# First graph layer: the score row taken by a block transpose on VectorE and a trip through DRAM instead of transposes on TensorE

## The chip, the cores and the metric

The kernel runs on one core of a Trainium2 chip. The metric is the time of one execution on the device, in microseconds (us). The kernel before takes 2509.26 us, the median of three runs (2508.89 to 2510.26 us).

## The reference

`x` is 64 graphs of 256 nodes with 512 features, all float32; `adj` is one 256 x 256 adjacency matrix for all graphs. Two layers follow each other, each with a residual:

```python
h = relu(layernorm(x)); x = x + layer0(h, adj)     # graph attention, 1 head
h = relu(layernorm(x)); x = x + layer1(h, adj)     # multi-head attention, 8 heads of 64

# layer0, per graph (W: 512 x 256, a: 2 x 256)
h  = X @ W
e  = (h @ a[0]) + (h @ a[1]).T         # a column plus a row: 256 x 256 scores
e  = leaky_relu(e, 0.2); masked softmax over neighbours -> alpha
out = concat([alpha @ h, h])
```

The change concerns `e` of the first layer: the sum of a column (a number per node, on the partitions) and a row (the same number of the other nodes, along the free dimension and equal on all partitions).

## The kernel before, in words

**Work units.** Two graphs make a group `g`; there are 32 groups (`NG`). A group has four tiles of 128 nodes (`GT = 4`), two per graph. The kernel is a software pipeline written out by hand: while the attention of group `g` runs (two halves, `b = 0` and `b = 1`, one per graph), the projections q, k, v of group `g+1` and the first layer of group `g+2` are fed into TensorE between its pieces. Each of these is a Python generator; one call of `next` emits one piece. The strings in `steps` say in which order the pieces are emitted: `S` scores of the second layer, `m` a mask of two heads, `u` one projection product (eight TensorE instructions of 256 columns pairwise, a piece of `project`), `o` an output product (`py`, a piece of `outputs`), `s` a piece of `first_layer`, `n` a piece of `first_norm` (the layernorm and transpose of a later group). TensorE follows this order exactly. For the other engines `not_sooner` ties an instruction to the one before it on its engine; where it is not used, a scheduler may place the instruction sooner or later.

**The first layer.** `first_layer(g)` has 14 pieces. Four pieces compute the head product `ph` of a tile: `h` with two more columns for the two scores; ScalarE copies it to `H` (`scalar.copy(H[:, r, : F1 + 2], ph)`), GpSimd adds it to the residual. The fifth piece makes the scores: four TensorE transposes into a PSUM tile `pn`, each of one column of `H` broadcast to 128 columns, which gives the row on all partitions; then four ScalarE instructions that add the column to it (`e<-pn,H`, 128 x 256), one leaky ReLU per graph on VectorE (`SCALAR_TENSOR_TENSOR e<-e`) and one exponential per graph on ScalarE (`ACTIVATE e<-e`). The sixth piece masks `e` on VectorE, the next four are the products `po`, and the last four normalise for the second layer.

**The order of one group's first half.** With `b = 0` the string is `Smmnuuuumonmuouuossnunosunosnouso`. Its last three pieces are a projection product `u`, the score piece `s` (`pn` and `e`), and an output product `o`. Then `weigh` of the half follows: eight products `total` (softmax sums), two VectorE reciprocals `r<-total`, two blocks `pr` of sixteen products, the products `oT` of `pr` and `r` on VectorE; and then the scores `sc` of the next half, eight banks of two products each, written in pairs and read by eight ScalarE exponentials `p<-sc`.

**PSUM.** Eight banks: three are held by name (`held_bank`), and five form the pool `turn` from which `mm` takes a bank for every other product. A product that takes a bank must wait until the bank's last reader is done. `ph`, `pn`, `total`, `pr`, `sc`, `po` and the second banks of the projections and outputs all come from these five. Which of the five a product gets is fixed when the program is built.

**Queues.** All loads and stores are issued by SyncE, one queue, in program order: an issue that waits holds the later ones. The first layer's norm already sends its tiles through DRAM (`passed`, `moved`). `r`, the tile of the reciprocals, has one buffer (`bufs=1`).

```python
for quad in range(NQ):
    not_sooner(vector, "reciprocal", r[:, quad, :], total[:, quad, :])
```

Of the kernel before, what the change touches and what calls it, by code (L numbers as in the profile page):

```python
# [8 lines left out]
F32 = mybir.dt.float32  # L9
I32 = mybir.dt.int32  # L10
AF = mybir.ActivationFunctionType
# [3 lines left out]
P = 128  # L15
# [26 lines left out]
def two_gnn_layers(tc, *args):  # L42

    nc = tc.nc
    with tc.tile_pool(name="verdict", bufs=1) as pool:
        wrong = pool.tile([1, 1], I32, name="wrong")
        bounded(tc, *args, wrong)  # L50
        again = nc.values_load(wrong[0:1, 0:1], min_val=0, max_val=1)
        with tc.If(again > 0):
            tc.strict_bb_all_engine_barrier()
            any_inputs(tc, *args)
# [3 lines left out]
def bounded(  # L58
# [23 lines left out]
    nc = tc.nc  # L82
    vector, scalar, gpsimd, sync = (
        Remembers(e) for e in (nc.vector, nc.scalar, nc.gpsimd, nc.sync)
    )
    B, N, D = x.shape
# [3 lines left out]
    NT = N // P  # L90
    GB = 2
    GT = GB * NT
    TOK = GB * N
# [3 lines left out]
    S = 32  # L97
# [4 lines left out]
    att = ctx.enter_context(tc.tile_pool(name="att", bufs=2))  # L102
    small = ctx.enter_context(tc.tile_pool(name="small", bufs=6))
    psum = ctx.enter_context(tc.tile_pool(name="psum", bufs=1, space=bass.MemoryType.PSUM))
    dram = ctx.enter_context(tc.tile_pool(name="dram", bufs=4, space=bass.MemoryType.DRAM))
# [3 lines left out]
    def mm(name):  # L109
        return psum.tile([P, 512], F32, tag="turn", name=name, bufs=5)  # L110
# [4 lines left out]
    def after(instruction, name):  # L115

        tc.add_manual_dep(
            instruction.ins, name,
            mybir.DependencyInfo(mybir.DependencyClass.NoSync, mybir.DependencyReason.DATA),
            reason="the engine's order",  # L120
        )

    def not_sooner(engine, operation, *args, **kwargs):

        last = engine.last
        after(getattr(engine, operation)(*args, **kwargs), last)
# [4 lines left out]
    def in_order(instruction):  # L131
        if before:
            after(instruction, before.pop())
        before.append(instruction.ins.name)

    def matmul(*args, **kwargs):
        in_order(nc.tensor.matmul(*args, **kwargs))  # L137

    def transpose(*args):
        in_order(nc.tensor.transpose(*args))  # L140
# [17 lines left out]
    ident = const.tile([P, P], F32, name="ident")  # L158
# [238 lines left out]
    def stats(mv, src, t, name):  # L397
        st = small.tile([P, 6], F32, tag="st", name=f"st{name}_{t}", bufs=4)
        if vector.last:
            not_sooner(vector, "bn_stats", st, src[t])  # L400
        else:
            vector.bn_stats(st, src[t])
        vector.bn_aggr(mv[:, t, :], st)
# [69 lines left out]
    def operand_sums(engine, quads, sums):  # L473
        a11, a12, a21, a22 = quads
        not_sooner(engine, "tensor_add", sums[:, 0], a21, a22)
        engine.tensor_sub(sums[:, 1], sums[:, 0], a11)

        not_sooner(engine, "tensor_sub", a21, a11, a21)
        engine.tensor_sub(sums[:, 2], a12, sums[:, 1])

    def seven(quads, sums):

        a11, a12, s3, a22 = quads
        s1, s2, s4 = (sums[:, i] for i in range(3))
        return {
            1: (a11, W11), 2: (a12, W21), 3: (s4, W22), 4: (a22, T4),
            5: (s1, T1), 6: (s2, T2), 7: (s3, T3),  # L490
        }
# [41 lines left out]
    H = const.tile([P, GT, F1 + 3], F32, name="H")  # L533
    gpsimd.memset(H[:, :, F1 + 2 :], 1.0)

    def first_layer(g):

        xt = [xs[g, b][:, t, :] for b in range(GB) for t in range(NT)]
        for r in range(GT):
            b, t = divmod(r, NT)  # L540
            ph = mm(f"ph_{g}_{r}")[:, : F1 + 2]
            for c in range(HP):
                matmul(
                    ph, hT0[g, b][:, c, t * P : (t + 1) * P], w0_sb[:, c, :],
                    start=(c == 0), stop=(c == HP - 1),
                )
            scalar.copy(H[:, r, : F1 + 2], ph)
            gpsimd.tensor_add(xt[r][:, F1:], H[:, r, 2 : F1 + 2], xt[r][:, F1:])
            yield

        pn = mm(f"pn_{g}")
        for t in range(GT):
            transpose(pn[:, t * P : (t + 1) * P], H[:, t, 0:1].to_broadcast([P, P]), ident)
        pT = {}
        for b in range(GB):
            e = att.tile([P, NT, N], F32, tag="e", name=f"e_{g}_{b}")
            for kb in range(NT):
                scalar.activation(
                    e[:, kb, :], pn[:, b * N : (b + 1) * N], AF.Identity,
                    bias=H[:, b * NT + kb, 1:2], scale=1.0,  # L560
                )
            vector.scalar_tensor_tensor(e, e, ALPHA, e, op0=ALU.mult, op1=ALU.max)
            scalar.activation(e, e, AF.Exp)
            pT[b] = e
        if g:
            yield
        for b in range(GB):
            not_sooner(vector, "tensor_mul", pT[b], pT[b], maskT)
        yield
        if g == 0:  # L570
            yield
        mv = small.tile([P, GT, 2], F32, tag="mv", name=f"mv1_{g}", bufs=4)
        factors, norm, turn, fetch, put = norm_T(xt, mv, f"1_{g}", g == 0)
        row_factors = small.tile([P, GT], F32, tag="ri", name=f"ri_{g}", bufs=2)
        for r in range(GT):
            b, t = divmod(r, NT)
            po = mm(f"po_{g}_{r}")[:, : F1 + 1]
            for kb in range(NT):
                matmul(
                    po, pT[b][:, kb, t * P : (t + 1) * P], H[:, b * NT + kb, 2:],  # L580
                    start=(kb == 0), stop=(kb == NT - 1),
                )
            ri = row_factors[:, r : r + 1]
            not_sooner(vector, "reciprocal", ri, po[:, F1:])
            vector.scalar_tensor_tensor(
                xt[r][:, :F1], po[:, :F1], ri, xt[r][:, :F1], op0=ALU.mult, op1=ALU.add
            )
            stats(mv, xt, r, f"1_{g}")
            if r == 1:
                factors(0)  # L590
            elif r == 2:
                norm(0)
            elif r == 3:
                factors(1)
                if g:
                    turn(0)
                    fetch(0)
            yield
        hT = big.tile([P, HP, TOK], F32, tag="hT1", name=f"hT1_{g}")
        sums = big.tile([P, 3, 2, N], F32, tag="sums", name=f"sums_{g}", bufs=1)  # L600
        quads = [
            hT[:, 2 * c : 2 * c + 2, r * N : (r + 1) * N] for r in range(2) for c in range(2)
        ]
        operands[g] = seven(quads, sums)
        if g == 0:
            turn(0)
            put(0, hT[:, :, :N])
            yield
        norm(1)
        yield  # L610
        turn(1)
        fetch(1)
        yield
        if g:
            put(0, hT[:, :, :N])
            yield
        put(1, hT[:, :, N:])
        operand_sums(gpsimd, quads, sums)
        yield
# [218 lines left out]
    for piece in range(5):  # L838
        next(norms)
        if piece == 3:  # L840
            score_columns()
            next(edges)
    products, pieces = project(0), first_layer(1) if NG > 1 else iter(())
    for piece, _ in enumerate(first_layer(0)):
        if piece == 1:
            next(norms)
            next(norms)
            next(edges)
        elif piece == 2:
            next(norms)  # L850
        elif piece == 3:
            next(norms)
            late_loads()
        elif piece == 4 or piece == 9:
            next(verdict)
        elif piece == 10:
            next(verdict)
            next(verdict)
            next(norms)
            next(norms)  # L860
            weight_sums("q")
        elif piece == 11:
            next(products)
            next(products)
# [18 lines left out]
    run(verdict)  # L883


    steps = ("Smmnuuuumonmuouuossnunosunosnouso", "Ssmmususuososmuomssusuonusonuouunous")
    waiting, late = None, iter(())
    for g in range(NG):
        products = project(g + 1) if g + 1 < NG else iter(())
        pieces = first_layer(g + 2) if g + 2 < NG else iter(())  # L890
        for b, parts in enumerate(steps):
            if g == b == 0:
# [401 lines left out]
```

## Time and profile before

| | |
|---|---|
| median of three runs | 2509.26 us |
| the profiled execution: time, and span in the trace | 2508.17 us, 2506.5 us |
| TensorE busy | 2473.7 us (99%) |
| VectorE, ScalarE, GpSimd busy | 1684.0, 1009.8, 1018.9 us |
| DMA, mean share of its engines, by tenths | 2 to 3 tenths in most slices |
| length of one group in the middle of the run | 76.4 us |

Busy time counts an engine's instructions; a wait shows in the profile as idle time before an instruction, with the engine that ended it. The chain of waits is followed back from the last instruction of the run, and says which engine's work sets the end. A timeline gives the start and the length of merged rows of equal instructions. An instruction's recorded length overlaps the next one's by its pipeline, so the start of the next is the better measure of how long it holds its engine.

### The profile page before, as it was taken

The page shows a single profiled execution, that of the slowest core. Times are in us where ns is not written, and L with a number is a line of the kernel's source. Part 1 is how long each engine was busy: PE and PEld are TensorE (multiplying, and loading weights), DVE is VectorE, ACT ScalarE, POOL GpSimd, SP SyncE. Part 2 cuts the span into 40 slices and gives each one's busy share as a digit, 9 for nine tenths or more (in the row PEclk, how much of TensorE's full clock was granted, in tenths as well). Part 3 has the DMA queues.
Part 4 walks back from the last instruction along what each step waited for, and adds up shares of the span by engine and source line. Part 5 has one row for each costly group of instructions (what it writes and reads, how often), then busy time and mean ns, then how long its engine had stood idle before and what let it go on. Part 6 is the DMA issues. An engine that isn't in the chain of part 4 may idle for free.

```text
span 2506.5 us, 41385 instructions
## 1 busy us (share of the span) xinstructions
PE 2473.7 (99%) x16158; PEld 2054.6 (82%) x16158; DVE 1684.0 (67%) x2971; ACT 1009.8 (40%) x2019; POOL 1018.9 (41%) x978
## 2 busy tenths in 40 slices
PE   8999999999999999999999999999999999999998
PEld 7778888888888888888888888888888888888886
DVE  6666766776667767667766667676677666676656
ACT  5533443443434434434434444344334344343321
POOL 3533434434444334444344443344443344433432
PEclk9999999999999999999999999999999999999999
DMA  5222222322232321222222323222222223232100
GB/s 189 68 85 69 67 93 81 97 74 81 73 96 82 101 74 63 92 85 93 77 84 68 101 76 102 74 69 86 85 93 84 77 68 101 76 101 75 51 28 35
DMA packets 129352, 205.39 MB, mean 82 GB/s; under 512 B 13952, under 2 KB 78208, under 8 KB 129152
## 3 DMA queue, kind: packets, MB, share of 16 engines
q1 hardware_dynamic: 129152, 202.69, 25.1%
q8 instruction: 129, 2.11, 0.4%
q14 instruction: 71, 0.58, 0.1%
HBM read 104.08 MB, written 98.57 MB: 81 GB/s over the span
## 4 chain that ended last, share of the span: by engine, by line
PE 96%; DVE 2%; DMA 1%; ACT 0%; issue 0%; POOL 0%; SPq 0%; ACTq 0%; DVEq 0%; POOLq 0%
PE pq L137 16%; PE pk L137 15%; PE py L137 15%; PE pv L137 15%; PE sc L137 10%; PE ph L137 9%; PE pr L137 8%; PE po L137 4%; PE total L137 3%; PE pn L140 1%; DMA moved<-passed 0%; DVE p L35 0%; DVE st L35 0%; DVE r L35 0%; DVE x L35 0%
## 5 line engine op out<-in xcount | busy, mean ns | idle before, releaser
L35 POOL TENSOR_TENSOR p<-p 128x512 f32<-128x512 f32 x256 | 410.2, 1617 | 688.0 <-DVE p L35 688.0
L35 DVE TENSOR_TENSOR x<-py,x 128x256 f32<-128x256 f32 x448 | 187.3, 418 | 409.5 <-PE py L137 400.8
L35 DVE TENSOR_TENSOR p<-p,maskT 128x1024 f32<-128x1024 f32 x256 | 341.3, 1354 | 0.0
L35 ACT ACTIVATE p<-sc 128x512 f32<-128x512 f32 x512 | 257.7, 624 | 195.6 <-PE sc L137 191.6
L35 ACT ACTIVATE xn<-x,factor 128x512 f32<-128x512 f32 x256 | 194.4, 807 | 202.3 <-POOL factor L35 202.3
L35 DVE RECIPROCAL r<-total 128x256 f32<-128x256 f32 x128 | 215.5, 1725 | 73.7 <-PE total L137 73.7
L137 PE MATMUL py<-wo_sb,oT 128*128 128x256 f32 x1024 | 262.4, 379 | 1.7 <-DVE x L35 1.1
L137 PE MATMUL sc<-q,k 64*128 64x256 f32 x2048 | 257.7, 389 | 0.8 <-DVE r L35 0.5
L137 PEld LDWEIGHTS sc<-q,k 64*128 64x128 f32 x2048 | 215.5, 186 | 43.5 <-issue 26.3
L137 PE MATMUL pk<-hT,wk_sb 128*128 128x256 f32 x1024 | 244.9, 382 | 0.0
L137 PE MATMUL pv<-wv_sb,hT 128*128 128x256 f32 x1024 | 238.3, 381 | 6.1 <-ACT kept_v L35 6.1
L137 PE MATMUL pq<-hT,wq_sb 128*128 128x256 f32 x1024 | 239.9, 382 | 0.0
L137 PE MATMUL ph<-w_sb,hT 128*128 128x258 f32 x1024 | 239.6, 381 | 0.3 <-ACT hT L35 0.3
L137 PE MATMUL pr<-p,v 128*32 128x256 f32 x4096 | 232.7, 379 | 0.0
L137 PEld LDWEIGHTS pv<-wv_sb,hT 128*128 128x128 f32 x1024 | 195.1, 191 | 33.5 <-ACT kept_v L35 6.9
L137 PEld LDWEIGHTS pk<-hT,wk_sb 128*128 128x128 f32 x1024 | 191.7, 190 | 36.1 <-issue 10.8
L137 PEld LDWEIGHTS pq<-hT,wq_sb 128*128 128x128 f32 x1024 | 191.8, 190 | 35.0 <-issue 9.9
L137 PEld LDWEIGHTS ph<-w_sb,hT 128*128 128x128 f32 x1024 | 194.3, 190 | 29.8 <-ACT hT L35 0.9
L137 PEld LDWEIGHTS py<-wo_sb,oT 128*128 128x128 f32 x1024 | 193.9, 190 | 29.9 <-DVE x L35 1.5
L35 POOL TENSOR_TENSOR factor<-factor,rexp 128x2 f32<-128x2 f32 x128 | 91.6, 716 | 289.8 <-DVE factor L35 289.8
L137 PEld LDWEIGHTS pr<-p,v 128*32 128x32 f32 x4096 | 133.1, 110 | 87.9
L137 PE MATMUL py<-wo_sb,o_sums 128*128 128x256 f32 x768 | 198.0, 380 | 3.6 <-DVE x L35 3.6
(122 smaller groups left out, 3665.6 us busy)
## 6 DMA issues: line engine op xcount, KB each, us to landing
passed<-xt SPq DMA_DIRECT2D x124, 512.0 KB, 2.8
moved<-passed SPq DMA_DIRECT2D x496, 128.0 KB, 3.2
x<-in_x_dram SPq DMA_DIRECT2D x64, 512.0 KB, 4.3
out_dram<-x SPq DMA_DIRECT2D x64, 512.0 KB, 3.1
wq_sb<-in_L_gnn_Wq_dram SPq DMA_DIRECT2D x2, 512.0 KB, 9.4
wk_sb<-in_L_gnn_Wk_dram SPq DMA_DIRECT2D x2, 512.0 KB, 10.7
wv_sb<-in_L_gnn_Wv_dram SPq DMA_DIRECT2D x2, 512.0 KB, 7.5
wo_sb<-in_L_gnn_Wo_dram SPq DMA_DIRECT2D x8, 128.0 KB, 3.9
```

Of the source, the lines that this page charges most:

```text
L35: instruction = getattr(self.engine, operation)(*args, **kwargs)
L137: in_order(nc.tensor.matmul(*args, **kwargs))
L140: in_order(nc.tensor.transpose(*args))
```

## The change

The four transposes into `pn` go for all groups but the first. In the piece of the fourth head product, VectorE transposes the first eight columns of `H` of all four tiles in blocks of 32 x 32 (`rows`, one instruction); SyncE stores 16 of its partitions, 32 numbers each, to a DRAM tile `line` (2 KB) and loads them back to all 128 partitions as `own` (256 KB). `own` lies in the buffer of the reciprocals `r`. The score additions read `own` in place of `pn`, and each is tied to the instruction before it on ScalarE (`not_sooner`). The order string of the first half changes: head products stand in two pairs, the first pair and two projection products sooner.

```diff
-            yield
-
-        pn = mm(f"pn_{g}")
-        for t in range(GT):
-            transpose(pn[:, t * P : (t + 1) * P], H[:, t, 0:1].to_broadcast([P, P]), ident)
+            if r < GT - 1:
+                yield
+
         pT = {}
+        if g:
+
+            rows = small.tile([P, GT, 8], F32, tag="rows", name=f"rows_{g}", bufs=2)
+            not_sooner(vector, "transpose", rows.rearrange("p t c -> p (t c)"), H[:, :, 0:8])
+            line = dram.tile([P // 8, S], F32, tag="line", name=f"line_{g}")
+            nc.sync.dma_start(line, rows.rearrange("p t c -> p (t c)")[::8, :])
+            own = att.tile([P, P // S, GT, S], F32, tag="r", name=f"own_{g}", bufs=1)
+            nc.sync.dma_start(
+                own.rearrange("p k t j -> p (k t j)"),
+                line.rearrange("(o k) j -> o (k j)", o=1).to_broadcast([P, TOK]),
+            )
+            own = own.rearrange("p k t j -> p t k j")
+            yield
+        else:
+            yield
+            pn = mm(f"pn_{g}")
+            for t in range(GT):
+                transpose(pn[:, t * P : (t + 1) * P], H[:, t, 0:1].to_broadcast([P, P]), ident)
+            own = pn.rearrange("p (t k j) -> p t k j", t=GT, j=S)
         for b in range(GB):
-            e = att.tile([P, NT, N], F32, tag="e", name=f"e_{g}_{b}")
+            e = pT[b] = att.tile([P, NT, N], F32, tag="e", name=f"e_{g}_{b}")
             for kb in range(NT):
-                scalar.activation(
-                    e[:, kb, :], pn[:, b * N : (b + 1) * N], AF.Identity,
+                not_sooner(
+                    scalar, "activation",
+                    e[:, kb, :].rearrange("p (t k j) -> p t k j", t=NT, j=S),
+                    own[:, b * NT : (b + 1) * NT], AF.Identity,
                     bias=H[:, b * NT + kb, 1:2], scale=1.0,
                 )
             vector.scalar_tensor_tensor(e, e, ALPHA, e, op0=ALU.mult, op1=ALU.max)
             scalar.activation(e, e, AF.Exp)
-            pT[b] = e
...
-    steps = ("Smmnuuuumonmuouuossnunosunosnouso", "Ssmmususuososmuomssusuonusonuouunous")
+    steps = ("Smmnuuuumonmuossnuussounounonouso", "Ssmmususuososmuomssusuonusonuouunous")
```

More of the change, by code (lines that the diff above doesn't have):

```diff
@@ L548, in first_layer @@
             gpsimd.tensor_add(xt[r][:, F1:], H[:, r, 2 : F1 + 2], xt[r][:, F1:])
-            yield
-        pn = mm(f"pn_{g}")
-        for t in range(GT):
-            transpose(pn[:, t * P : (t + 1) * P], H[:, t, 0:1].to_broadcast([P, P]), ident)
-        pT = {}
+            if r < GT - 1:
+                yield
+        pT = {}
+        if g:
[9 more added lines that the diff above has]
+            own = own.rearrange("p k t j -> p t k j")
+            yield
+        else:
[4 more added lines that the diff above has]
+            own = pn.rearrange("p (t k j) -> p t k j", t=GT, j=S)
         for b in range(GB):
-            e = att.tile([P, NT, N], F32, tag="e", name=f"e_{g}_{b}")
+            e = pT[b] = att.tile([P, NT, N], F32, tag="e", name=f"e_{g}_{b}")
             for kb in range(NT):
-                scalar.activation(
-                    e[:, kb, :], pn[:, b * N : (b + 1) * N], AF.Identity,
+                not_sooner(
+                    scalar, "activation",
+                    e[:, kb, :].rearrange("p (t k j) -> p t k j", t=NT, j=S),
+                    own[:, b * NT : (b + 1) * NT], AF.Identity,
                     bias=H[:, b * NT + kb, 1:2], scale=1.0,
```

## The prediction

> **What bounds the kernel now.** I read the busy line first, then the chain of waits by engine, then one group's timeline.
>
> ```profile
> PE 2473.7 (99%) x16158; PEld 2054.6 (82%) x16158; DVE 1684.0 (67%) x2971; ACT 1009.8 (40%) x2019; POOL 1018.9 (41%) x978
> ...
> PE 96%; DVE 2%; DMA 1%; ACT 0%; issue 0%; POOL 0%; SPq 0%; ACTq 0%; DVEq 0%; POOLq 0%
> ```
>
> TensorE is full: the other engines count only where they make it wait, and it has no idle time in which a new wait could hide. A microsecond taken off TensorE is a microsecond won; one of new waiting is lost. The place of the change, in the timeline of a group in the middle (start, length, engine, row):
>
> ```profile
> 1203.85 0.60 PE L140 MATMUL pn<-ident,H 128*128 128x128 f32 x4
> 1204.06 0.84 ACT L35 ACTIVATE kept_k<-pk,bk_sb 128x256 f32<-128x256 f32 x2 [2.22 <-PE pk L137]
> ...
> 1204.29 1.03 PE L137 MATMUL py<-wo_sb,o_sums 128*128 128x256 f32 x4
> 1204.78 1.57 ACT L35 ACTIVATE e<-pn,H 128x256 f32<-128x256 f32 x4
> ...
> 1205.70 1.38 DVE L35 SCALAR_TENSOR_TENSOR e<-e 128x512 f32<-128x512 f32 x2
> ...
> 1206.14 3.64 PE L137 MATMUL pr<-p,v 128*32 128x256 f32 x64
> 1206.41 1.33 ACT L35 ACTIVATE e<-e 128x512 f32<-128x512 f32 x2
> 1206.99 3.36 DVE L35 RECIPROCAL r<-total 128x256 f32<-128x256 f32 x2
> ...
> 1209.70 4.11 PE L137 MATMUL sc<-q,k 64*128 64x256 f32 x32
> 1210.27 1.22 DVE L35 TENSOR_TENSOR oT<-pr,r 128x512 f32<-128x512 f32 x2
> 1210.87 4.03 ACT L35 ACTIVATE p<-sc 128x512 f32<-128x512 f32 x8 [3.13 <-PE sc L137]
> ```
>
> Three things are to be seen. `pn` holds TensorE 0.44 us (1203.85 to 1204.29). The two leaky ReLUs stand on VectorE directly ahead of the reciprocals: whatever makes `e` late makes those late. And the reciprocals end at 1210.35, while the third `sc` bank, which reuses `total`'s, starts at 1209.70 + 4 x 0.2525 = 1210.71 (16 products in the 4.04 us to the next row at 1213.74): the slack is **0.36 us**.
>
> **What the Trainium skill says.** "VectorE: DVE Perf Modes", The three transpose paths: VectorE transposes within 32 x 32 blocks only. That is why 16 rows of 32 numbers have to be collected through DRAM; the trace's 128 x 512 transposes take 694 ns, and show no more of it. "DMA: Bandwidth & Descriptors", Anatomy of one DMA, puts the fixed part at about 2 us (for GpSimd's path); here SyncE's smallest transfers land in as much, 2.0 us. Its Rules for kernel authors ask for an outermost dimension that is a multiple of 16 so that a transfer uses all 16 engines; `own`'s is 128. No run here separates that.
>
> **The change part by part.**
>
> *Transposes gone.* 30 groups have this place (first layers of groups 2 to 31): 30 x 0.44 = 13.2 us off TensorE. Group 1's is worked out below, group 0 keeps its own.
>
> *The row's way.* Let R be the end of the last head product. ScalarE's copy of H ends at R + 0.55 (0.2 start, 0.37 long). `rows` has 32 columns against 512 in 694 ns; tiny VectorE rows take 0.14 to 0.2, I take 0.2: R + 0.8, bounds 0.14 to 0.7. It stands in VectorE's order ahead of an output addition whose product ends only at R + 0.87, so it delays nothing. SyncE: `line` and `own` are issued in 0.35 and 0.4 us ahead of `passed` of a later group, which is ready only near R + 8; the loads and stores behind have tens of us (this `passed` is fetched 40 us later). Landing times are in the DMA view:
>
> ```profile
> b_out<-in_L_gnn_bo_dram SPq DMA_DIRECT2D x1, 256.0 KB, 4.5
> bv_col<-in_L_gnn_bv_dram SPq DMA_DIRECT2D x8, 0.2 KB, 2.0
> ```
>
> `b_out` is the same broadcast of 2 KB to 128 partitions. So `own` lands at R + 0.8 + 0.1 + 2.0 + 0.1 + 4.5 = R + 7.5; with `a_b`'s 6.9 (a like load amid the start's traffic) at R + 9.9; with 3 us at R + 6. From R to the score piece the new string has four outputs (0.87 each) and three projections (1.73): 8.65 us; the last projection's eviction holds ScalarE until 0.92 later (1203.85 to 1204.78). The additions are due at R + 9.6: the row is hidden by 2 us, at worst 0.3 late.
>
> *The order on ScalarE: the step that decides.* Before, it runs four additions, then two exponentials. Built with `not_sooner`, the changed program's order is: two additions, exponential of graph 0, two additions, exponential of graph 1. The exponential waits for VectorE's leaky ReLU, so the second graph's additions now wait for the first graph's round trip. From the start s of the additions (1204.78 before; it hangs on the eviction of the last projection, which does not move): additions to s + 0.85 (0.36 + 0.484); ReLU 0 from s + 0.91 to s + 1.60 (0.692); exponential 0 s + 1.62 to 2.25 (0.629); the additions of graph 1 from s + 2.12 (exponentials follow each other in 0.49) to s + 2.97; ReLU 1 s + 3.02 to 3.71; reciprocals from s + 3.62. Before: s + 2.21. They are **1.41 us later** and end at s + 6.98, or 1211.76.
>
> *Where TensorE waits for it.* With `pn` gone all its work stands 0.44 earlier: `sc` from 1209.26. The third bank would be due at 1210.27. In the changed program's bank allocation the third `sc` reuses the first `sc`'s bank and the fourth takes `total`'s. The first exponential of `sc` starts 1.17 after the `sc` row (1210.87 - 1209.70) and lasts 0.617: 1211.08 with 0.03 for the release, a wait of 0.81. The fourth is then due at 1211.33 and waits for the reciprocals until 1211.80: 0.47. The fifth to eighth find their banks free (`oT` ends at 1212.33 and 1212.90; those banks are due at 1212.8 and 1213.6). Sum of waits 1.28; less 0.44 the group is **0.84 us longer**. `po` needs the masked `e`, ready at 1214.98, due at 1216.4. VectorE runs 1.3 late here and regains its place in the 0.44 us idle at 1222.7. 30 x 0.84 = **25.2 us**.
>
> *Start, group 1.* Here the score piece follows its head products by one projection only. The copy of H ends at 63.78; `own` lands at 63.78 + 0.2 + 0.1 + 2.0 + 0.1 + 4.5 = 70.7, where the additions started at 65.91. The chain above needs 4.45 us to the second exponential (75.1), then four squares of 0.54 stand ahead on ScalarE of the sum that VectorE does before the mask (77.3), and the mask takes 0.69: `po` at 78.0 against 72.25, **+5.8 us**; bounds 1 (a landing in 3 us, the rest regained in later waits) and 8. Group 0: the second graph's chain is 1.3 later, of which TensorE's other work hides some: +0.4, bounds 0 and 0.8.
>
> *Edits at nothing.* The additions read SBUF for PSUM: 128 x 512 copies take 0.57 from SBUF and 0.56 from PSUM. The `r` buffer: `own`'s last reader precedes the ReLU that precedes the reciprocals on VectorE anyway. The head products in pairs: the first starts 4.3 us sooner (`uuo` moved behind), its operand was 5.7 ready ahead; the second pair has the two projections, 3.46 us, to cover the copy of its operand, which needs 1.1.
>
> *Sum.* 25.2 + 5.8 + 0.4 = 31.4 us. Against the profiled execution's own 2508.17 (span 2506.5 and 1.7 around it) that is 2539.6; the median shown is 1.1 higher: **2540.7 us**.
>
> **The rivals.** About 0.2%, 5 us, is what can be told from no change.
>
> *Only the bank wait shows (0.12).* The second graph's chain is shorter or partly overlaps, and the reciprocals are not last. Then 0.81 - 0.44 = 0.37 a group: 11 + 6, about 2526 us. Against it: the order on ScalarE is fixed.
>
> *The row is late (0.14).* `own` lands after its turn on ScalarE, and the whole chain with it. `a_b`'s 6.9 us speaks for it, `b_out`'s 4.5 against. A full us late costs 30 more: 2571 us.
>
> *Faster (0.07).* The waits at `sc` do not bind, because ScalarE starts the exponentials earlier than the second `sc` product suggests and the ReLU follows sooner. It turns where the waits together fall below 0.44 us a group, the place of `pn`; with none, -13.2 + 5.8: about 2502 us. Against it: the slack of 0.36 is measured, and TensorE has no other idle time. That the change does not remove `pn` is ruled out: the built program has none after the first group.
>
> **How the numbers follow.** The likeliest case, delay as worked, has 0.67, with its own range 2522 to 2558 (half a us a group either side at most, start 1 to 8). The range 2516 to 2566 leaves out the faster case and the farther part of the late row. Faster by over 0.2%: 0.07; within: 0.03; slower: 0.90.
>
> **What would show it.** In the profile after: no `pn` in the groups; ScalarE's `e` rows as two, one, two, one; reciprocals 1.4 us later after the first addition; TensorE idle before `sc` released by ScalarE `p` and VectorE `r`, some 38 us in all; about 77.3 us a group; `own` landing in 3 to 5 us. Wrong if `sc` shows no idle time, or if the additions of `e` wait for the DMA in each group: then the row was not hidden.

## The result, and the profile after

The changed kernel takes **2545.57 us** (median of four runs, 2545.31 to 2546.06) against 2509.15 us for the kernel before in the same session: a ratio of 1.0145 with a 95% interval of 1.0127 to 1.0162, slower by 36.4 us. The forecast was 2540.7 us, slower. The profiled execution after has a span of 2543.7 us (2506.5 before) at a granted TensorE clock of 0.997 (the share of the full clock that the trace shows as granted to TensorE; 0.999 before).

From the page of the kernel after: the busy line, the chain of waits by engine, the group of score products (busy us, mean ns of one, then the idle time just before them and what ended it).

```profile
PE 2482.0 (98%) x16034; PEld 2038.4 (80%) x16034; DVE 1680.7 (66%) x3002; ACT 1020.4 (40%) x2019; POOL 1018.7 (40%) x978
...
PE 86%; DVE 7%; ACT 4%; issue 2%; DMA 1%; POOL 0%; SPq 0%; ACTq 0%; DVEq 0%; POOLq 0%
...
L137 PE MATMUL sc<-q,k 64*128 64x256 f32 x2048 | 275.2, 390 | 25.1 <-ACT p L35 20.5
```

TensorE has 124 instructions fewer (16158 to 16034: four transposes in 31 groups), and yet 8.3 us more of recorded busy time. The chain no longer lies almost wholly on TensorE: VectorE has 7% and ScalarE 4%, where they had 2% and 0%. The `sc` row now has 25.1 us of idle time before it (0.8 before), most of it ended by the exponential `p`.

The same place in a group in the middle, from the timeline of the kernel after (start, length, engine, row):

```profile
1217.66 0.35 SPq L560 DMA_DIRECT2D own<-line  x1
...
1224.00 0.84 ACT L35 ACTIVATE kept_k<-pk,bk_sb 128x256 f32<-128x256 f32 x2 [2.91 <-PE pk L137]
1224.73 0.90 ACT L35 ACTIVATE e<-own,H 128x256 f32<-128x256 f32 x2
...
1225.66 0.69 DVE L35 SCALAR_TENSOR_TENSOR e<-e 128x512 f32<-128x512 f32 x1 [0.38 <-ACT e L35]
1226.39 0.63 ACT L35 ACTIVATE e<-e 128x512 f32<-128x512 f32 x1 [0.76 <-DVE e L35]
1226.92 0.89 ACT L35 ACTIVATE e<-own,H 128x256 f32<-128x256 f32 x2
1227.85 0.69 DVE L35 SCALAR_TENSOR_TENSOR e<-e 128x512 f32<-128x512 f32 x1 [1.49 <-ACT e L35]
1228.46 3.36 DVE L35 RECIPROCAL r<-total 128x256 f32<-128x256 f32 x2
...
1229.21 1.13 PE L137 MATMUL sc<-q,k 64*128 64x256 f32 x8
...
1230.37 1.08 ACT L35 ACTIVATE p<-sc 128x512 f32<-128x512 f32 x2 [1.17 <-PE sc L137]
...
1231.02 0.70 PE L137 MATMUL sc<-q,k 64*128 64x256 f32 x2 [0.68 <-ACT p L35]
1231.74 1.22 DVE L35 TENSOR_TENSOR oT<-pr,r 128x512 f32<-128x512 f32 x2
...
1231.88 2.85 PE L137 MATMUL sc<-q,k 64*128 64x256 f32 x22 [0.16 <-DVE r L35]
...
1234.66 1.56 PE L137 MATMUL pk<-hT,wk_sb 128*128 128x256 f32 x6
```

Read it from s = 1224.73. The additions come in two pairs, with exponential 0 between them (1226.39). VectorE sits idle 1.49 us before ReLU 1, and the reciprocals start at 1228.46, s + 3.73, where before they started at s + 2.21. The first two banks of `sc` run from 1229.21. By the prediction's spacing of 0.2525 us a product the third is due 1.01 us later; it starts at 1231.02, 0.80 late, when the first bank's exponential is done. The fourth is due at 1231.27 and starts at 1231.88, 0.61 late, after the reciprocal. That makes 1.41 us, and the whole row agrees: from its start to the next product it takes 5.45 us (1229.21 to 1234.66), where it took 4.04. The brackets show only 0.68 and 0.16: a row's modelled length runs into the wait behind it, so starts have to be compared, not brackets. `own` is issued at 1217.66 and lands 3.2 us later (median), 3.9 us before its use.

The 37.2 us between the two spans divide by the first score addition of a group: 6.7 us are there at group 2 (134.32 for 127.62); 27.9 us come in the 29 groups to group 31 (2385.65 for 2351.09, so 34.6 by then), 0.96 each; 2.6 us come after, group 31's own and somewhat over 1 us of a stretch at a granted clock of 0.58 (2522 to 2525).

### The profile page after: what moved, and what is told of

It reads as the page before. It is cut to its first block, busy times and chain, and to the rows that moved or that the text cites. A ratio compares the mean times of both kernels' runs of the same rounds, so it can differ in the third digit from the quotient of the medians.

```text
span 2543.7 us, 41289 instructions
## 1 busy us (share of the span) xinstructions
PE 2482.0 (98%) x16034; PEld 2038.4 (80%) x16034; DVE 1680.7 (66%) x3002; ACT 1020.4 (40%) x2019; POOL 1018.7 (40%) x978
## 4 chain that ended last, share of the span: by engine, by line
PE 86%; DVE 7%; ACT 4%; issue 2%; DMA 1%; POOL 0%; SPq 0%; ACTq 0%; DVEq 0%; POOLq 0%
PE pq L137 15%; PE pk L137 15%; PE pv L137 14%; PE py L137 14%; PE ph L137 9%; PE sc L137 8%; PE pr L137 4%; PE po L137 4%; DVE r L35 4%; ACT e L35 3%; PE total L137 1%; DVE e L35 1%; ACT kept_k L35 1%; DMA moved<-passed 0%; DVE st L35 0%
## 5 line engine op out<-in xcount | busy, mean ns | idle before, releaser
L137 PE MATMUL sc<-q,k 64*128 64x256 f32 x2048 | 275.2, 390 | 25.1 <-ACT p L35 20.5
L137 PEld LDWEIGHTS sc<-q,k 64*128 64x128 f32 x2048 | 208.6, 186 | 92.3 <-ACT p L35 33.3
```

## Experiments

Below, s is the start of the first score addition, and "period" the length of a group in the middle: 76.42 us before, 77.40 after. ReLU 0 and ReLU 1 are the leaky ReLUs of a group's two graphs, and exponential 0 and 1 their exponentials. The recorded expectations name some runs by labels: e1 has all four additions first, e2 the tie alone, e7 and e8 the additions untied, e11 the reciprocal asked to go first.

### The tie alone, in the kernel before

```diff
-                scalar.activation(
+                not_sooner(
+                    scalar, "activation",
                     e[:, kb, :], pn[:, b * N : (b + 1) * N], AF.Identity,
```

> The kernel before, with pn, the old string and no trip through DRAM; only the score additions are tied on ScalarE as in the change. Theory (the tie makes graph 1's additions wait for graph 0's ReLU and exponential, and VectorE's reciprocals with them): reciprocals 1.4 to 1.5 us later after the first addition, TensorE idle at sc 1.2 to 1.5 us in each of 30 groups: 2545 to 2556 us, as slow as the whole change or slower. Rival (the row's trip through DRAM or the new string costs the time): no change, 2509 us.

Measured: 2512.63 us, ratio 1.001 (1.0003 to 1.0017). Not what I expected: the period stays 76.42 us. The timeline of this kernel:

```profile
1210.26 0.84 ACT L35 ACTIVATE e<-pn,H 128x256 f32<-128x256 f32 x2
...
1211.18 0.68 DVE L35 SCALAR_TENSOR_TENSOR e<-e 128x512 f32<-128x512 f32 x1
...
1211.87 1.76 DVE L35 RECIPROCAL r<-total 128x256 f32<-128x256 f32 x1
...
1212.43 0.82 ACT L35 ACTIVATE e<-pn,H 128x256 f32<-128x256 f32 x2
1213.54 0.63 DVE L35 SCALAR_TENSOR_TENSOR e<-e 128x512 f32<-128x512 f32 x1
1214.09 1.75 DVE L35 RECIPROCAL r<-total 128x256 f32<-128x256 f32 x1
```

ScalarE's order is the changed kernel's (two additions, exponential, two additions), but the scheduler has put the first reciprocal between the ReLUs, into the very time that VectorE idles in the kernel after. The second ends at s + 5.58, as before. So the tie alone costs 2.7 us against the kernel before of the same session (2509.95), and is not enough; something must hold both reciprocals behind ReLU 1.

### The same, with both ReLUs made to come first

The tie as above; the first reciprocal is also tied to the last leaky ReLU that was emitted, ReLU 1.

```diff
+    relu = {}
...
+            relu[0] = vector.last
...
-            not_sooner(vector, "reciprocal", r[:, quad, :], total[:, quad, :])
+            last = vector.last
+            inverse = vector.reciprocal(r[:, quad, :], total[:, quad, :])
+            after(inverse, last)
+            if quad == 0:
+                after(inverse, relu[0])
```

> As e2 (the kernel before with the tie alone, where VectorE ran one reciprocal between the two ReLUs), but both ReLUs ahead of both reciprocals on VectorE, as in the change. Theory, mended (it takes the tie and this order on VectorE together): reciprocals 1.4 us later, TensorE waits at sc some 1.1 to 1.2 us more in each of 30 groups, 2541 to 2548 us. Rival (neither order matters; the DRAM trip or the bank allocation of the change costs the time): 2513 us as e2.

Measured: 2542.57 us, ratio 1.0131 (1.0114 to 1.0148). The timeline:

```profile
1222.19 0.84 ACT L35 ACTIVATE e<-pn,H 128x256 f32<-128x256 f32 x2
...
1225.21 0.69 DVE L35 SCALAR_TENSOR_TENSOR e<-e 128x512 f32<-128x512 f32 x1 [1.42 <-ACT e L35]
1225.82 3.36 DVE L35 RECIPROCAL r<-total 128x256 f32<-128x256 f32 x2
...
1229.33 2.92 PE L137 MATMUL sc<-q,k 64*128 64x256 f32 x24 [1.08 <-DVE r L35]
```

Here are the changed kernel's order on VectorE, reciprocals at s + 3.63 and a wait of TensorE at `sc`, with `pn` still in place and no row through DRAM. Tie and order together carry 32.5 of the 36.4 us (2542.57 against 2510.08 us for the kernel before in the same session). The banks are not those of the changed kernel: here the third `sc` bank waits for the reciprocals, and no bank before it for an exponential `p`. The time is lost all the same, so the changed kernel's other choice of banks isn't its cause.

### The row in another buffer, tie kept

`own` takes the buffer of `hT0` for the groups from 2 on.

```diff
-            own = att.tile([P, P // S, GT, S], F32, tag="r", name=f"own_{g}", bufs=1)
+            pool, tag = (big, "hT0") if g > 1 else (att, "r")
+            own = pool.tile([P, P // S, GT, S], F32, tag=tag, name=f"own_{g}", bufs=1)
```

> The change, tie and all, but own lies in the buffer of hT0 (free at that time) and not in that of the reciprocals. The scheduler then puts the first reciprocal between the two ReLUs by itself, and the third sc reuses total's bank. Theory, mended by e11 (the tie costs only because the reciprocals may not overwrite own before graph 1's additions have read it): first reciprocal some 1.6 us after the first addition, second ended at about 5.6, about 76.5 us a group, 2515 to 2520 us as e1. Rival (the tie alone costs it): 2540 us or more.

Measured: 2516.75 us, ratio 1.0032 (1.0019 to 1.0044), 29 us under the changed kernel; the period is 76.34 us. The timeline:

```profile
1211.45 0.90 ACT L35 ACTIVATE e<-own,H 128x256 f32<-128x256 f32 x2
...
1212.39 0.69 DVE L35 SCALAR_TENSOR_TENSOR e<-e 128x512 f32<-128x512 f32 x1 [0.38 <-ACT e L35]
1213.00 1.75 DVE L35 RECIPROCAL r<-total 128x256 f32<-128x256 f32 x1
...
1214.66 0.63 DVE L35 SCALAR_TENSOR_TENSOR e<-e 128x512 f32<-128x512 f32 x1
1215.21 1.75 DVE L35 RECIPROCAL r<-total 128x256 f32<-128x256 f32 x1
```

With the row out of `r`'s buffer, the scheduler puts the first reciprocal between the ReLUs again (s + 1.55). The reciprocals write the buffer that graph 1's additions read, so in the changed kernel they may not start before those additions have read it; that is what holds them. The choice of banks differs here too (the third bank is `total`'s again), but the run before this one lost its time with that choice as well.

### Buffer kept, reciprocal asked to go first

ReLU 1 and exponential 1 of groups 2 to 31 are put off (`put_off`) and emitted after the first reciprocal.

```diff
+    put_off = []
...
-            vector.scalar_tensor_tensor(e, e, ALPHA, e, op0=ALU.mult, op1=ALU.max)
-            scalar.activation(e, e, AF.Exp)
+
+            def rest(e=e):
+                not_sooner(vector, "scalar_tensor_tensor", e, e, ALPHA, e, op0=ALU.mult, op1=ALU.max)
+                not_sooner(scalar, "activation", e, e, AF.Exp)
+
+            if g > 1 and b:
+                put_off.append(rest)
+            else:
+                rest()
...
             not_sooner(vector, "reciprocal", r[:, quad, :], total[:, quad, :])
+            while put_off:
+                put_off.pop()()
```

> The change, tie and all, but with VectorE's first reciprocal between the two ReLUs. Its third sc still reuses the first sc's bank, its fourth total's. Theory: the wait for the reciprocals (about half a us a group) goes, the wait of the third sc for ScalarE (0.8 us) stays: about 76.8 us a group, 2525 to 2532 us. Rival (the reciprocals are the whole wait): 2510 to 2518 us as e1. Rival (VectorE's order is not the cause): 2545 us.

Measured: 2548.41 us, ratio 1.0157 (1.014 to 1.0174); no gain, a miss. The timeline:

```profile
1225.64 0.90 ACT L35 ACTIVATE e<-own,H 128x256 f32<-128x256 f32 x2
...
1227.84 0.89 ACT L35 ACTIVATE e<-own,H 128x256 f32<-128x256 f32 x2
1228.76 1.76 DVE L35 RECIPROCAL r<-total 128x256 f32<-128x256 f32 x1 [1.50 <-ACT e L35]
...
1230.44 0.63 DVE L35 SCALAR_TENSOR_TENSOR e<-e 128x512 f32<-128x512 f32 x1
...
1230.98 1.74 DVE L35 RECIPROCAL r<-total 128x256 f32<-128x256 f32 x1
```

The order of the code was obeyed, but the first reciprocal waits 1.50 us, and the wait ends 0.03 after graph 1's additions: it is the shared buffer that it waits for. I had reckoned with VectorE's order and left the buffer out. With ReLU 1 now between the two, the second reciprocal ends at s + 7.08, as in the changed kernel (s + 7.09), and the period is the same, 77.39 us. Exponential 1 now comes late too, ahead of ScalarE's exponentials of `sc`.

### All four additions first, buffer kept

The changed kernel with the four additions, tied, ahead of ReLUs and exponentials, as the kernel before runs them.

```diff
         for b in range(GB):
             e = pT[b] = att.tile([P, NT, N], F32, tag="e", name=f"e_{g}_{b}")
...
+        for b in range(GB):
+            e = pT[b]
             vector.scalar_tensor_tensor(e, e, ALPHA, e, op0=ALU.mult, op1=ALU.max)
-            scalar.activation(e, e, AF.Exp)
+            not_sooner(scalar, "activation", e, e, AF.Exp)
```

> The change with ScalarE's order of before: four additions, then the two exponentials, all tied. Theory: reciprocals 2.2 to 2.3 us after the first addition again. TensorE, 0.44 us earlier without pn, then waits about as much at sc, because VectorE did not get earlier: 76.4 to 76.6 us a group, and some 5 to 6 us more at the start: 2512 to 2519 us. Rival (the row comes late): still about 77.4 us a group, 2540 us or more.

Measured: 2517.75 us, ratio 1.0031 (1.002 to 1.0043); period 76.54 us, reciprocals at s + 2.34. The loss is gone although the buffer is shared. But there is no gain either, though `pn` is out. From the timeline:

```profile
1210.58 1.70 ACT L35 ACTIVATE e<-own,H 128x256 f32<-128x256 f32 x4
...
1212.92 3.36 DVE L35 RECIPROCAL r<-total 128x256 f32<-128x256 f32 x2
...
1215.07 1.13 PE L137 MATMUL sc<-q,k 64*128 64x256 f32 x8
...
1216.43 3.31 PE L137 MATMUL sc<-q,k 64*128 64x256 f32 x24 [0.23 <-DVE r L35]
```

`sc` starts at s + 4.49 where it started at s + 4.92 before, and then waits for the reciprocals, which did not come sooner. What TensorE saved ahead of VectorE's chain, it waits for behind it.

### How much slack the kernel before had there

One more VectorE instruction of 0.68 us on the mask (it changes no value) ahead of the reciprocals, in groups 2 to 31.

```diff
+        if g > 1:
+            not_sooner(vector, "tensor_tensor", maskT, maskT, maskT, op=ALU.max)
```

> The kernel before with one more VectorE instruction of 128 x 512 (maskT as the maximum of itself and itself, 0.69 us) between the ReLUs and the reciprocals in 30 groups. If the slack of 0.36 us at the third sc were the only one that counts, TensorE would wait 0.33 us a group: 2519 us. If the fourth sc, which reuses a pr bank and starts 0.04 us after oT ends, has none: 0.65 us a group, 2528 to 2531 us.

Measured: 2528.09 us, ratio 1.0073 (1.0056 to 1.009). The reciprocals start 0.61 us later (s + 2.82), the period is 0.60 longer: no slack at all. The prediction's 0.36 us is that of the third bank. The fourth takes one of `pr`'s banks and waits for `oT`, the last reader of `pr`. The single instructions of the traces show how long: in the fastest kernel below, where neither waits, the third and the fourth bank start side by side, 0.97 us after the first, so in the kernel before the fourth was due at 1209.70 + 0.97 = 1210.67. The first `oT` ends at 1210.90, and the fourth bank starts at 1210.96. The kernel before already waits there, by some 0.28 us.

### The additions untied, and group 1 as before

First the changed kernel with plain `scalar.activation`; then the same with `pn` kept in group 1.

```diff
-                not_sooner(
-                    scalar, "activation",
+                scalar.activation(
```

> The change without the tie: the scheduler puts the four additions ahead of the last projection's eviction on ScalarE. Theory: own has landed by then (3.2 us landing), the reciprocals wait for total alone, no idle time at sc, pn's 0.44 us are won in 30 groups: 13 less, 3 to 6 more at the start, 2499 to 2503 us. Rival (the row comes late): the additions wait for the DMA and hold the eviction behind them, 2530 us or more.

Measured: 2495.16 us, ratio 0.9938 (0.9922 to 0.9955), 4 us under the range I gave.

```diff
-        if g:
+        if g > 1:
```

> The untied change (e7), with group 1 as well keeping its transposes into pn. Theory: what the trip through DRAM cost at the start (a wait of some 4 us ahead of po and the slower clock after it) goes: 5 to 7 us under e7, 2488 to 2490 us. Rival (the start's loss is regained in later waits): 2495 us as e7.

Measured: 2492.07 us, ratio **0.993 (0.9913 to 0.9946)**: faster than both kernels, 18 us under the kernel before in the same session (2510.08) and 53 under the changed one. The period is 75.79 us in both. The timeline of the second:

```profile
1191.26 0.34 SPq L560 DMA_DIRECT2D own<-line  x1
...
1194.57 1.69 ACT L35 ACTIVATE e<-own,H 128x256 f32<-128x256 f32 x4
...
1196.86 1.27 DVE L35 SCALAR_TENSOR_TENSOR e<-e 128x512 f32<-128x512 f32 x2
...
1197.59 0.84 ACT L35 ACTIVATE kept_k<-pk,bk_sb 128x256 f32<-128x256 f32 x2 [1.32 <-PE pk L137]
...
1199.48 3.37 DVE L35 RECIPROCAL r<-total 128x256 f32<-128x256 f32 x2 [0.61 <-PE total L137]
...
1202.80 3.92 PE L137 MATMUL sc<-q,k 64*128 64x256 f32 x32
```

Freed, the scheduler places the additions ahead of the last projection's eviction `kept_k` (ScalarE's copy of a product out of its bank), not behind it. The ReLUs are done before `total` is, the reciprocals wait for `total` alone, and `sc` is one row of 32 with no wait. VectorE's chain has come forward together with TensorE's, and so the 0.44 us of `pn` is won, and 0.19 us besides, by which the row of 32 is shorter than before (3.92 for 4.11): the wait at the fourth bank is gone too. That 0.19 in 30 groups is 5.7 us, about what the first of the two runs was faster than I expected. But the row is only just in time now: `own`, issued at 1191.26, lands 3.0 us later, a median 0.25 us before the additions, where the changed kernel leaves 3.9. Group 1's row was worth 3.1 us, about half of what I expected.

### The order string alone, and its part in hiding the row

The new string in the kernel before, then the old string in the fastest kernel:

> The kernel before with the new order string alone. Theory: the head products in pairs cost nothing, 2506 to 2512 us. Rival (the string makes products wait for operands or banks): over 2520 us, with idle time ahead of ph or of the projections.

Measured: 2509.35 us, ratio 0.9999 (0.999 to 1.0008): nothing by itself.

```diff
-    steps = ("Smmnuuuumonmuossnuussounounonouso", ...)
+    steps = ("Smmnuuuumonmuouuossnunosunosnouso", ...)
```

> The fastest so far (e8: no tie, group 1 keeps pn) with the old order string. The last head product ends one output and one projection (2.6 us) before the score piece, while the row needs about 5.7 us from there: the additions wait some 2.2 us for the DMA in 30 groups, and VectorE's reciprocals with them. Theory (the new string is what hides the row): about 78.7 us a group, 2570 to 2582 us. Rival (the string does not matter): 2492 to 2497 us.

Measured: 2616.56 us, ratio 1.0425 (1.0407 to 1.0442). From its timeline:

```profile
1261.55 1.71 ACT L35 ACTIVATE e<-own,H 128x256 f32<-128x256 f32 x4 [3.46 <-DMA own<-line]
```

In all 30 groups the additions wait for the row, 102.3 us together or 3.4 each, where I reckoned with 2.2; `own` lands in 4.3 us here, not in 3.2. That explains the sign, not the whole of the 124 us over the fastest kernel: these waits also made TensorE wait, and the run's mean clock was 0.986 against 0.997, which by my estimate is up to 29 us (0.014 of 2614 us against 0.003 of 2490). How the rest divides isn't shown. The string thus costs nothing and gives the row the time it needs.

### A longer way for the row

A second DRAM tile on the way in groups 2 to 31, tie and buffer as in the changed kernel.

```diff
+            if g > 1:
+                hop = dram.tile([P // 8, S], F32, tag="hop", name=f"hop_{g}")
+                nc.sync.dma_start(hop, line)
+                line = hop
```

> The change with one more copy of the row from DRAM to DRAM between line and own, in groups 2 to 31. own was landed 3.9 us before the additions; the hop takes about 2. Theory (the row is hidden): no change, 2543 to 2549 us. Rival (the row is on the path): some 2 us a group more, 2600 us.

Measured: 2551.12 us, ratio 1.0163 (1.0146 to 1.018), 2 us above the range I gave. The hop lands in 1.8 us, and the period is 77.41 us, as without it: in the steady state the row is hidden even so, and lands a median 2.0 us before its use. The difference lies at the start: the additions of group 2 are at 139.7 for 134.3, and one wait of 1.5 us for the DMA is in the trace.

### What group 1's row costs at the start

The changed kernel, tie and all, with `if g > 1:` as above.

> The changed kernel, but group 1 keeps the TensorE transposes into pn; groups 2 to 31 stand as in the changed kernel. It prices the start. Theory, by the changed kernel's trace (TensorE idle 4.35 us before group 1's po, and about 2.3 us lost to the halved clock after it, less some 1 us regained in other waits and some of the idle that pn itself brings): 5 to 6.5 us faster than the changed kernel, 2539 to 2541 us, with no stretch at half clock near 77 us. Rival, by what the same edit was worth without the tie (3 us): 2542 to 2543 us. If the start cost nothing: 2545 us. The group period in the middle stays at 77.4 us in each case.

Measured: 2541.65 us, ratio 1.0126 (1.0109 to 1.0143), 3.9 us under the changed kernel: between the theory's 5 to 6.5 and the rival's 3. The start's idle time and clock in the changed kernel, by stretches (stretch, length, busy time of PE, PEld, DVE, ACT, POOL with instructions, granted clock, DMA share, GB/s):

```profile
73.00:77.35 4.35, 0.00 (x1) 0.03 (x1) 1.59 (x4) 3.29 (x12) 0.00 (x0) 0.74 0.00 0
77.35:79.00 1.65, 1.65 (x4) 1.37 (x5) 1.06 (x2) 0.00 (x0) 0.00 (x0) 0.50 0.04 10
...
83.00:90.00 7.00, 7.00 (x35) 6.18 (x34) 6.21 (x26) 2.36 (x4) 3.48 (x4) 1.00 0.02 10
```

and the same place with `pn` in group 1:

```profile
73.00:77.00 4.00, 3.20 (x16) 2.51 (x15) 2.61 (x6) 1.83 (x7) 0.00 (x0) 1.00 0.02 4
77.00:79.00 2.00, 2.00 (x11) 1.77 (x10) 1.79 (x5) 0.00 (x0) 0.00 (x0) 1.00 0.00 0
```

TensorE idles 4.35 us before group 1's `po` and then runs at half its clock; with `pn` there are 0.80 us of idle and no drop. Part of the loss comes back in waits that the kernel before has later: 2.69 us for `kept_v` at 85.7, of which 1.95 are left after.

## Why the prediction was right, and where its steps were off

The runs of the first experiments side by side. The medians are of several sessions, in which the kernel before read 2509.15 to 2510.40 us.

| kernel | row | reciprocals may precede graph 1's additions | reciprocals start | period | median, us |
|---|---|---|---|---|---|
| before | `pn` | not needed, the additions come first | s + 2.21 | 76.42 | 2509.15 |
| before, tied | `pn` | yes | s + 1.61 | 76.42 | 2512.63 |
| before, tied, ReLUs first | `pn` | no, by order | s + 3.63 | 77.45 | 2542.57 |
| after | `own` in `r` | no, by the buffer | s + 3.73 | 77.40 | 2545.57 |
| after, `own` elsewhere | `own` in `hT0` | yes | s + 1.55 | 76.34 | 2516.75 |
| after, additions first | `own` in `r` | not needed, the additions come first | s + 2.34 | 76.54 | 2517.75 |

- **The path: right.** The order on ScalarE, later reciprocals and two waits of TensorE at `sc` were predicted at s + 3.62, 0.81 and 0.47; they measured s + 3.73, 0.80 and 0.61 by the same spacing of banks. The 0.11 lies in ScalarE's pairs (0.90 for the assumed 0.85) and the ReLUs behind them. The group is 0.96 to 0.98 longer where 0.84 was worked out: 29 us for 25.2 in 30 groups. That is most of the 5 us by which the forecast was low. The spacing was wrong, and luck hid it: the two banks of a pair are due together, so by starts the third waits 0.84 and the fourth 0.85, but the kernel before already had 0.28 of wait there, and 0.84 + 0.85 - 0.28 is the same 1.41.
- **"The order on ScalarE: the step that decides": half of it.** The tie alone costs 2.7 us; the shared buffer alone does no harm (additions first: reciprocals at s + 2.34; additions untied: faster than before). Only together do they hold both reciprocals behind ReLU 1. The prediction took that order from the changed program and so got the number, but it gave the reason wrongly.
- **"Edits at nothing: the `r` buffer": failed.** "`own`'s last reader precedes the ReLU that precedes the reciprocals on VectorE anyway" is true only as long as nothing moves; without the sharing the first reciprocal goes ahead of ReLU 1, and 29 us go with it.
- **The slack of 0.36 us: the wrong bank.** The slack that counts is that of the fourth bank, and it had none. The sum did not use it, but it supported the case against the "faster" rival.
- **"A microsecond taken off TensorE is a microsecond won": false at this place.** With all delay gone and `pn` out, the period was 76.54 and 76.34. TensorE was full, but it already waited for VectorE's chain at the fourth bank; only the untied additions, which moved both, won 0.63 us a group.
- **The row: hidden, with more room than I gave it.** `own` landed in 3.2 us, not in 4.5, and 3.9 us ahead of its use, not 2.1. "DMA: Bandwidth & Descriptors", Anatomy of one DMA, of the Trainium skill, was cited for some 2 us of fixed time on GpSimd's path. SyncE's 2 KB took 1.6 us to DRAM and 1.8 us from DRAM to DRAM, so that figure was somewhat long for this queue.
- **The start.** Group 0's `po` came 0.97 later (26.68 for 25.71), with 0.88 us of idle that the exponential of graph 1 ended; I had 0.4, bound 0.8. Group 1's row I put at 5.8; keeping `pn` there saves 3.9 (that kernel, tie and all, is still 2.9 late by group 2). The lateness itself was near (77.35 for 72.25, 1.0 of it carried over from group 0, so 4.1). I had no clock in that sum, nor what later waits give back. With both, the parts come to the 6.7 us by group 2: 1.0 and 4.1, some 2.3 for the clock (last section), less 0.7 at the wait for `kept_v`.
- **The rivals.** "Only the bank wait" (2526) fell: the fourth bank waits for `r`. "The row is late" fell: one wait for the DMA in group 1. "Faster" did not happen here, but is what the untied additions do, since with them its condition holds.

## What to carry to other kernels

Where a tile is put into another tile's buffer, ask which instructions may no longer pass each other: here that order, built in quietly with one tie on another engine, cost more than the removed work was worth. When work leaves the full engine, look whether the chain beside it that meets it next comes forward too; if it does not, the gain turns into a wait of the same size. A tie that forces an order is tried both ways, since the scheduler's own place for the additions was worth 50 us against the tied one (2495.16 for 2545.57).

## What was not expected of the hardware

The idle time of 4.35 us at the start halved TensorE's granted clock. By finer stretches of the changed kernel, in the same form as above:

```profile
73.00:75.13 2.13, 0.00 (x1) 0.00 (x0) 0.69 (x1) 1.34 (x5) 0.00 (x0) 1.00 0.00 0
75.13:77.35 2.22, 0.00 (x0) 0.03 (x1) 0.90 (x3) 1.95 (x8) 0.00 (x0) 0.50 0.00 0
77.35:81.96 4.61, 4.61 (x11) 3.69 (x12) 3.26 (x9) 0.00 (x0) 0.00 (x0) 0.50 0.01 4
81.96:83.00 1.04, 1.04 (x7) 0.91 (x6) 0.97 (x4) 0.00 (x0) 0.00 (x0) 1.00 0.00 0
```

"TensorE: Matmul & The Clock Gate", The HAM clock gate, of the Trainium skill says that the clock falls to half after an idle window of about 3.4 us and comes back after a busy one of the same length. The return agrees: it came 4.6 us after the work resumed, not sooner than 3.4. The fall fits less well: it came only 2.1 us into the idle time. In the kernel before, a wait of 4.87 us (for `kept_v`, ended at 166.36) had the clock still at 1.00 to its end, and it read 0.51 from 166.8 to 170.3. The measured times decide: in these two waits the length alone doesn't tell when the clock falls. A wait of this length costs more than itself: 4.61 us at 0.50 are 2.3 us of lost full-speed time.
